# Loads moved from SyncE's to GpSimd's queue, and a transpose moved behind the next row maxima

## The chip, the core and the metric

The kernel runs on one core of a Trainium2 chip. The metric is the device time of one execution in microseconds. The core has TensorE (PE in the profile: matrix products), VectorE (DVE), ScalarE (ACT), GpSimd (POOL) and SyncE (SP, which here only issues DMAs), each working through its own list of instructions in order.

## The reference

Two layers are applied to x of shape (8, 32, 32, 512), all in float32. The second layer is where the change lies; S is 1024 pixels of an image, C is 512.

```python
# layer 0: group norm, 8-head self-attention over the 1024 pixels of an image, residual
x = x + softmax(q k^T) v @ w_out + b_out          # q, k, v from group_norm(x) @ w_qkv + b_qkv
# layer 1: deformable attention
x_ln   = layernorm(x)
q      = x_ln (channels first, re-read as rows of 512) @ wq + bq
o      = gelu(depthwise_conv_7x7_stride_2(q) + dw_b)       # 16 x 16 points per image
grid   = ref_points + tanh(conv_1x1(o))
interp = bilinear_sample(x, grid)                           # 256 sampled rows per image
k = v  = interp @ wv + bv
attn   = softmax((q @ mq_w + mq_b)(k @ mk_w + mk_b)^T)      # 8 heads of 64, 256 keys
msa    = (attn @ (v @ mv_w + mv_b)) @ mo_w + mo_b
z      = msa + x
out    = gelu(layernorm(z) @ mlp_w + mlp_b) + z
```

## The kernel before

The first pass does layer 0 for all images; it leaves in DRAM the rows `mid` (the layer's output), the normalised rows `hat_d` and, for the first images, the convolution's sums `o_d`. The second pass is layer 1 and begins after 2.1 ms. Only the second pass is changed.

**Units.** The second pass goes through 16 half images `hi` of 512 query rows, and each half image through 4 pairs of heads. One pair of one half image is a unit; the units are numbered n = 0 to 63 and are called U0 to U63 here. `unit_steps` (line 1219) makes, for its pair: the scores against 256 keys on TensorE (tile `sc`), the row maxima on VectorE (`nmax`, two instructions), the exponentials on ScalarE (`e`), their transposes on VectorE (`sq`, two), a trip of the transposed tile through DRAM (`sq_d`, `et`), the reciprocal sums (`rs`, `rsT`, through DRAM into `inv`), the product with the values on TensorE (`av`, in the next unit), and its scaling on VectorE into `attH`.

**Behind the attention.** `back_steps` (line 1111) takes a finished half image 128 rows at a time, one such block t per unit. Its steps: `fetch` (DMA of the residual rows into `xr`), `add` (GpSimd adds a bias row to `xr`), `joined` (four-step product `mm<-wo,attH` on TensorE, sum with `xr` into `z` on VectorE, statistics `stats` and `mv`, with one power on GpSimd), `norm` (`zn` on VectorE), `away` (four DMAs `zn_d<-zn` into DRAM), `back` (the DMA `zn<-zn_d`, which brings the tile back with its 32x32 blocks exchanged), `blocks` (VectorE transposes within the blocks: `zT<-zn`), `mlp` (the product `mm<-wm,zT` on TensorE), `biased` (`res` on VectorE), `gelu` on ScalarE, and `end` (GpSimd adds `z` and stores). In the last block or so of the pass TensorE makes the turn instead, without `blocks`.

**Beside it.** For images 6 and 7 the depthwise convolution is made during the units. `conv_steps` (line 1248) runs it in two lanes: lane 0 is five taps per unit on VectorE (two in three of every eight units), each one instruction of `chunk<-pad,dww,chunk`; lane 1 is seven taps per unit, a product on ScalarE (`parts`) and an addition on GpSimd (`chunk<-parts,chunk`). `conv_fetch` (line 950) loads a `hat` for each of eight chunks. `point_steps` (line 1273) finds the sampling points of the next image once per eight units: `conv_load` (line 954) loads the sums `o`, some 24 very small VectorE instructions find the corners, GpSimd gathers rows (`row`, four indirect DMAs), and VectorE weighs them into `smp` (four instructions, in two units of every eight). `fetch_hat` (line 1078) loads the features `hat_h` of a half image for its query products `mm<-hat_h,wqq`.

**Order.** Every step is filed with a place, a decimal number in units, by `at(place, step)`; `run_due` carries all steps out in the order of their places. A wrapper (`InOrder`, line 54) keeps each engine's instructions in just that order. So the places are the order of each engine's list and of each DMA queue, and every instruction of the second pass stands in the profile under line 54: one goes by the tiles. A tile's pool has a fixed number of buffers; a write into a tile waits until the last reader of that buffer is done.

Within unit n the places that matter here are: scores and maxima n; `joined` n + 0.012; first `sq` n + 0.02; `norm` n + 0.03; `away` n + 0.0301; sums n + 0.039; `back` n + 0.0395; `biased` of the block before n + 0.0392; second `sq` n + 0.04; loading of `et` n + 0.0401; `inv` n + 0.0411; query product n + 0.042; `av` of the unit before n + 0.1; its scaling into `attH` n + 0.2; `blocks` n + 0.21; samples n + 0.22; lane 0 taps n + 0.25 on; `xr` loads n + 0.4 of every second unit; and `mlp` n + 1.03, in the next unit.

Of the kernel before, what the change touches and what calls it, by code (L numbers as in the profile page):

```python
# [17 lines left out]
P = 128  # L18
# [4 lines left out]
NC = C // P  # L23
# [224 lines left out]
def attention_then_deformable_attention(  # L248
# [30 lines left out]
    nc = tc.nc  # L279
# [15 lines left out]
    hat_d = [dram.tile([P, NT, C], F32, tag=f"hat{b}", name=f"hat_d{b}") for b in range(B)]  # L295
# [72 lines left out]
    def at(place, step):  # L368
        due.append((place, len(due), step))
# [9 lines left out]
    o_d = [dram.tile([P, NC, NS], F32, tag=f"o{b}", name=f"o_d{b}") for b in range(B)]  # L379
# [27 lines left out]
    with ExitStack() as l0:  # L407
# [3 lines left out]
        nc = InOrder(tc)  # L411
        NX = 2
        NX_T = 3
        xs = {}
# [380 lines left out]
        for b in range(B):  # L795
# [22 lines left out]
            for hp in range(NHP):  # L818
                for qt in range(NT):
                    n = first + hp * NT + qt  # L820
# [7 lines left out]
                    t = qkv[b, hp]  # L828
# [14 lines left out]
    with ExitStack() as l1:  # L843
        nc = tc.nc
# [9 lines left out]
        nc = InOrder(tc)  # L854
# [93 lines left out]
        chat, room = {}, {}  # L948

        def conv_fetch(b, cb):  # L950
            chat[b, cb] = cvhat.tile([P, NT, P], F32, tag="hat", name="hat", bufs=2)
            nc.sync.dma_start(chat[b, cb], hat_d[b][:, :, ts(cb, P)])

        def conv_load(b):
            room[b, "o"] = cv.tile([P, NC, NS], F32, tag="o", name="o")
            nc.sync.dma_start(room[b, "o"], o_d[b][:, :, :])

        def fill(b, cb, par):
            hat = chat[b, cb]
# [64 lines left out]
        def points(b):  # L1024
            conv_load(b)
            conv_gelu(b)
            offsets(b)
            offsets_turned(b)
            targets(b)
            for h in range(2):  # L1030
                gather(b, h)
                sample(b, h)
# [43 lines left out]
        hat, keys, vals, queries, attH = {}, {}, {}, {}, {}  # L1076

        def fetch_hat(hi):
            hat[hi] = raw.tile([P, NC, C], F32, tag="hat", name="hat_h", bufs=2)
            nc.sync.dma_start(hat[hi], hat_d[hi // 2][:, ts(hi % 2, NC), :])  # L1080

# [24 lines left out]
        def tmp(name, bufs):  # L1108
            return work.tile([P, C], F32, tag=name, name=name, bufs=bufs)

        def back_steps(hi, start, step, tail=False):

            b, half = divmod(hi, 2)
            xs = mid[b].rearrange("(t p e) c -> e t p c", e=2, p=P)[half]
            outs = out_tok[b].rearrange("(t p e) c -> e t p c", e=2, p=P)[half]
            xr, z, zn, zT, res = {}, {}, {}, {}, {}
            n_units = 2 * B * NHP

            def fetch(t):
                xr[t] = tmp("xr", 4)  # L1120
                nc.sync.dma_start(xr[t], xs[t])

            def add(t):
                nc.gpsimd.tensor_tensor(xr[t], xr[t], bo_row, ALU.add)
# [21 lines left out]
            def by_matmul(t):  # L1146
                return tail or start + step * t >= n_units - 1
# [42 lines left out]
            for t in range(NC):  # L1190
                over, eve = (start + step * t >= n_units - i and not tail for i in range(2))
                n, pair = start + step * t, start + step * (t - t % 2)

                ends = (n + 0.0301, n + 0.0395, n + 0.21, n + 1.03, n + 1.0392)
                if eve:
                    ends = (n + 0.61, n + 0.72, n + 0.73) if over else (n + 1.06, n + 1.62, n + 1.625)
                places = (pair - 2.6, pair - 1.45), (n + 0.012, n + 0.03), ends
                if tail:
                    turn = n + 0.15 + 0.005 * (t > 0)
                    places = (n - 0.7, n - 0.6), (n, n + 0.01), (turn, n + 0.25, n + 0.26)  # L1200
                turns = (turned,) if by_matmul(t) else (away, back, blocks)
                steps = (fetch, add), (joined, norm), (*turns, mlp, biased)
                for place, what in zip(sum(places, ()), sum(steps, ())):
                    at(place, lambda t=t, what=what: what(t))


                ends = [t - 1, t] if t % 2 and not tail else [t] if tail else []

                for what, after in (
                    (gelu, 0.27 if tail else 0.735 if over else 1.72),  # L1210
                    (end, 0.28 if tail else 0.74 if over else 2.0125),
                ):
                    for i in ends:
                        at(n + after, lambda i=i, what=what: what(i))
# [33 lines left out]
        def conv_steps():  # L1248
            for lane, chunks in enumerate(((0, 3, 6), (1, 2, 4, 5, 7))):
                free = 0.5 + lane  # L1250
                for k in chunks:
                    b, cb = EARLY + k // NC, k % NC
                    first = next(n for n in range(60) if n + 0.49 > free)
                    fills = [first + 0.49, first + 0.55]
                    at(fills[0] - 1.8, lambda b=b, cb=cb: conv_fetch(b, cb))
                    for par, place in enumerate(fills):
                        at(place, lambda b=b, cb=cb, par=par: fill(b, cb, par))
                        at(place + 0.02, lambda lane=lane, par=par: fill_end(lane, par))
                    unit = int(fills[1]) + 1
                    i = 0  # L1260
                    while i < KS * KS:
                        points = unit % (2 * NHP) in (NHP - 1, NHP, NHP + 2)
                        count = 7 if lane else 2 if points else 5
                        for j in range(count):
                            if i == KS * KS:
                                break
                            place = 0.25 + 0.01 * j if not lane else 0.045 + 0.001 * j if j < 4 else 0.65 + 0.01 * j
                            at(unit + place, lambda b=b, cb=cb, i=i, lane=lane: tap(b, cb, i, lane))
                            free = unit + place
                            i += 1  # L1270
                        unit += 1

        def point_steps(b):
            last = 2 * NHP * b - NHP
            at(last - 3.5, lambda: conv_load(b))
            at(last - 2.035, lambda: conv_gelu(b))
            at(last - 1.465, lambda: offsets(b))
            at(last - 1.36, lambda: offsets_turned(b))
            at(last - 0.959, lambda: targets(b))
            for h, (p0, p1) in enumerate(((-0.28, 0.22), (1.72, 2.22))):  # L1280
                at(last + p0, lambda h=h: gather(b, h))
                at(last + p1, lambda h=h: sample(b, h))
            first = 2 * NHP * b
            for hp, place in enumerate((-0.82, -0.815, 0.185, 1.18)):
                at(first + place, lambda hp=hp: key_step(b, hp))
            for t, place in enumerate((-0.81, 0.18)):
                at(first + place, lambda t=t: value_step(b, t))
# [22 lines left out]
        bq_row = wo = wm = bo_row = bm_row = None  # L1310
        prep()
        fetch_hat(0)
        fetch_hat(1)
        for hp in range(NHP):
            key_step(0, hp)
# [10 lines left out]
        for hi in range(2 * B):  # L1326
            if hi > 1:
                at(NHP * (hi - 1) - 1, lambda hi=hi: fetch_hat(hi))
            if hi + 1 < 2 * B:
                back_steps(hi, NHP * (hi + 1) + 1, 1)  # L1330
            else:
                back_steps(hi, NHP * (hi + 1) + 0.65, 0.1, tail=True)
# [34 lines left out]
```

## Time and profile before

| | us |
|---|---|
| median of 3 runs | 3410.59 (3407.61 to 3411.03) |
| the profiled execution | 3415.02 |
| its span from first to last instruction | 3413.3 |
| PE busy | 3274.7 (96%) |
| DVE busy | 2505.4 (73%) |
| ACT busy | 1776.7 (52%) |
| POOL busy | 1537.2 (45%) |

The profile is one execution; busy times are shares of its span. In a row of a timeline the columns are start in us, duration in us, engine, line, operation, out<-in tiles with shapes, and how many instructions are merged (xN); a bracket gives the idle time of the engine before the first of them and what ended it. A row of waits says which engine waited for what: us in total, how many times, the longest. `SPq` and `POOLq` are the queues of those engines, on which DMAs are issued. The granted TensorE clock was 0.983 of full speed on average.

### The profile page before, as it was taken

To read this page: it belongs to the slowest core of one execution; us is meant where nothing else is said; L and a number is where in the kernel's file an instruction comes from. 1 tells how busy PE (TensorE), PEld (TensorE's weight loads), DVE (VectorE), ACT (ScalarE), POOL (GpSimd) and SP (SyncE) were. 2 spreads that over 40 slices of the span, in tenths; PEclk is the share of its full clock that TensorE was granted. 3 is DMA by queue.
4 is the path that set the end of the run, shared out by engine and by line. 5 is a ranking of instruction groups with operands and counts; after the bars stand their busy time and mean duration, and the time that the engine had idled before them with its cause. 6 is when DMAs were issued, how large, how long until landed. Compare 5 with 4: busy or idle time off the path is not lost. (4 is left out here: it accounts for less than half of the span.)

```text
span 3413.3 us, 59709 instructions
## 1 busy us (share of the span) xinstructions
PE 3274.7 (96%) x21504; PEld 1330.2 (39%) x21504; DVE 2505.4 (73%) x3431; ACT 1776.7 (52%) x3811; POOL 1537.2 (45%) x1903
## 2 busy tenths in 40 slices
PE   7999999999999999999999997989999999989998
PEld 3444444444444444444344343433333333333333
DVE  5776788888888888888888885166757767655664
ACT  3443365576576576576566561245544555544342
POOL 1002226646646746745745663114545354532322
PEclk9999999999999999999999999899999999999999
DMA  5666766766766766766776766466667676777764
GB/s 154 176 178 165 207 179 199 214 175 188 221 178 181 229 183 181 217 189 178 212 195 179 209 183 199 130 183 223 213 195 235 222 225 212 227 226 223 249 212 144
DMA packets 488551, 673.01 MB, mean 197 GB/s; under 512 B 81888, under 2 KB 275424, under 8 KB 486208
## 3 DMA queue, kind: packets, MB, share of 16 engines
q1 hardware_dynamic: 457616, 567.09, 57.7%
q0 software_dynamic: 29488, 100.00, 9.6%
q8 instruction: 171, 2.80, 0.3%
q10 hardware_dynamic: 1152, 2.10, 0.2%
q14 instruction: 124, 1.02, 0.1%
HBM read 261.59 MB, written 138.94 MB: 117 GB/s over the span
## 5 line engine op out<-in xcount | busy, mean ns | idle before, releaser
L54 ACT ACTIVATE e<-sc,nmax 128x1024 f32<-128x1024 f32 (+1 forms) x1024 | 802.4, 797 | 606.6 <-DVE nmax L54 605.0
L54 DVE TENSOR_REDUCE nmax<-sc 128x1 f32<-128x1024 f32 (+1 forms) x640 | 751.2, 1214 | 244.8 <-PE sc L54 244.1
L54 POOL TENSOR_TENSOR oa<-part_x,oa 128x256 f32<-128x256 f32 x852 | 639.1, 750 | 556.0 <-ACT part_x L54 509.6
L54 DVE STREAM_TRANSPOSE sq<-e 128x1024 f32<-128x1024 f32 x640 | 766.2, 1228 | 133.6 <-ACT e L54 113.6
L54 ACT ACTIVATE part_x<-pad_x,dww_x 128x256 f32<-128x256 f32 x852 | 440.6, 544 | 243.3 <-POOL oa L54 242.3
L54 PE MATMUL sc<-k,q 64*64 64x512 f32 x4096 | 516.8, 604 | 12.5 <-ACT e L54 9.3
L54 PE MATMUL av<-et,v 128*64 128x256 f32 x4096 | 501.8, 387 | 18.8 <-DMA et<-sq 8.6
L54 PE MATMUL mm<-xT,wqkv 128*64 128x512 f32 x2048 | 463.7, 595 | 3.2 <-issue 3.2
L54 PEld LDWEIGHTS av<-et,v 128*64 128x64 f32 x4096 | 275.8, 137 | 336.3 <-issue 172.4
L54 POOL TENSOR_TENSOR mv<-mv,minus_half 128x1 f32<-128x1 f32 x128 | 76.4, 597 | 605.8 <-DVE mv L54 605.3
L54 PE MATMUL mm<-wm,zT 128*64 128x512 f32 x1024 | 252.7, 639 | 49.8 <-DVE zT L54 48.7
L54 POOL TENSOR_TENSOR chunk<-parts,chunk 128x256 f32<-128x256 f32 x240 | 180.7, 753 | 207.8 <-ACT parts L54 193.4
L54 PEld LDWEIGHTS sc<-k,q 64*64 64x64 f32 x4096 | 137.9, 132 | 321.8 <-issue 207.5
L54 PEld LDWEIGHTS mm<-xT,wqkv 128*64 128x64 f32 x2048 | 149.6, 138 | 254.5 <-issue 239.4
L54 PE MATMUL mm<-wo,attH 128*64 128x512 f32 x1024 | 235.0, 599 | 3.6 <-DVE pad L54 3.6
L54 DVE SCALAR_TENSOR_TENSOR od<-pad_x,dww_x,od 128x256 f32<-128x256 f32 x276 | 233.7, 847 | 5.5
L54 PE MATMUL mm<-wqkv,xT 128*64 128x256 f32 x2048 | 232.1, 379 | 0.0
L54 PE MATMUL mm<-hat_h,wqq 128*64 128x512 f32 x1024 | 231.2, 593 | 0.0
L54 PE MATMUL mm<-w,attT 128*64 128x512 f32 x1024 | 229.8, 592 | 1.4 <-DVE attT L54 1.4
L54 ACT ACTIVATION_READ_ACCUMULATOR e<-sc,nmax 128x1 f32 x1024 | 209.3, 204 | 0.0
L54 DVE STREAM_TRANSPOSE zT<-zn 128x512 f32<-128x512 f32 x58 | 41.3, 711 | 207.6 <-DMA zn<-zn_d 207.6
L54 ACT ACTIVATE parts<-pad,dww 128x256 f32<-128x256 f32 x240 | 126.6, 549 | 115.9 <-POOL chunk L54 115.7
(165 smaller groups left out, 3402.8 us busy)
## 6 DMA issues: line engine op xcount, KB each, us to landing
et<-sq SPq DMA_DIRECT2D x2048, 128.0 KB, 2.8
sq_d<-sq SPq DMA_DIRECT2D x128, 512.0 KB, 3.8
et<-sq_d SPq DMA_DIRECT2D x128, 512.0 KB, 5.1
inv<-rs_d SPq DMA_DIRECT2D x256, 128.0 KB, 4.6
hat_h<-hat_d SPq DMA_DIRECT2D x16, 1024.0 KB, 7.8
xr<-mid SPq DMA_DIRECT2D x64, 256.0 KB, 5.5
x<-in_x_dram POOLq DMA_DIRECT2D x60, 256.0 KB, 4.5
out_dram<-res POOLq DMA_DIRECT2D x60, 256.0 KB, 3.2
```

The costliest lines, as they stand in the source:

```text
L54: return self.tc.keep_in_program_order(op(*args, **kwargs))
```

## The change

The second pass's loads of `hat` (`conv_fetch`, 8 of them), `o` (`conv_load`, 8), `hat_h` (`fetch_hat`, 14 of 16: all but the first two) and `xr` (`fetch`, 64) are issued on GpSimd's queue and not on SyncE's, at the same places. And `blocks`, the transpose `zT<-zn`, goes from place n + 0.21 to n + 1.011. In VectorE's list it stood behind the scaling into `attH` and ahead of the samples and taps; it now stands behind samples, taps and the two maxima of the next unit, and ahead of that unit's `z`. TensorE's list stays as it was, and ScalarE's too.

```diff
@@ conv_fetch, conv_load
-            nc.sync.dma_start(chat[b, cb], hat_d[b][:, :, ts(cb, P)])
+            nc.gpsimd.dma_start(chat[b, cb], hat_d[b][:, :, ts(cb, P)])
...
-            nc.sync.dma_start(room[b, "o"], o_d[b][:, :, :])
+            nc.gpsimd.dma_start(room[b, "o"], o_d[b][:, :, :])
@@ fetch_hat
-            nc.sync.dma_start(hat[hi], hat_d[hi // 2][:, ts(hi % 2, NC), :])
+            (nc.gpsimd if hi > 1 else nc.sync).dma_start(hat[hi], hat_d[hi // 2][:, ts(hi % 2, NC), :])
@@ back_steps, fetch
-                nc.sync.dma_start(xr[t], xs[t])
+                nc.gpsimd.dma_start(xr[t], xs[t])
@@ back_steps, the places of away, back, blocks, mlp, biased
-                ends = (n + 0.0301, n + 0.0395, n + 0.21, n + 1.03, n + 1.0392)
+                ends = (n + 0.0301, n + 0.0395, n + 1.011, n + 1.03, n + 1.0392)
```

## The prediction

> **What bounds it now.** First I read the busy shares: PE has work in 96% of the span, and in the second pass nothing else comes near (VectorE 66% and GpSimd 42% over 2300 to 3300 us). So what counts there is PE's idle time and slow products. The table of waits over 2300 to 3413 us (engine, line, releaser; us, times, longest) says what the change can touch:
>
> ```profile
> DVE zT L54 <- DMA zn<-zn_d: 207.6, 58, 7.7
> DVE attH L54 <- PE av L54: 59.6, 28, 3.3
> PE mm L54 <- DVE zT L54: 48.7, 18, 6.4
> ```
>
> VectorE loses 207.6 us with `zT` at the head of its list and `zn` still on the way; PE pays 48.7 us of it. Second, PE's timeline where nothing is late (U58):
>
> ```profile
> 3276.16 1.96 PE L54 MATMUL sc<-keys,q 64*64 64x256 f32 x32
> 3278.04 3.65 PE L54 MATMUL mm<-wo,attH 128*64 128x512 f32 x16
> 3281.53 3.60 PE L54 MATMUL mm<-wm,zT 128*64 128x512 f32 x16
> 3284.96 3.60 PE L54 MATMUL mm<-hat_h,wqq 128*64 128x512 f32 x16
> 3288.39 1.89 PE L54 MATMUL av<-et,vals 128*64 128x512 f32 x8
> 3290.21 1.96 PE L54 MATMUL sc<-keys,q 64*64 64x256 f32 x32
> ```
>
> A clean unit is 14.05 us, start to start, and the product that needs `zT` is due 1.88 + 3.49 = 5.37 us after `av` has ended (more where PE has keys, values or a convolution fill in between; call that E). Compare a stalled one, PE's row and VectorE's at the same time:
>
> ```profile
> 2792.17 6.33 PE L54 MATMUL mm<-wm,zT 128*64 128x512 f32 x16 [4.56 <-DVE zT L54]
> ```
> ```profile
> 2791.31 0.71 DVE L54 STREAM_TRANSPOSE zT<-zn 128x512 f32<-128x512 f32 x1 [4.47 <-DMA zn<-zn_d]
> ```
>
> It pays twice: 4.56 us of idle time, and a product of 6.33 us where 3.60 is normal; in 100-us stretches with such stalls the granted clock is 0.95 to 0.97 instead of 1.00. Over the 18 waits the slow products add 21.7 us. The most that removing them all can give is 48.7 + 21.7, some 70 us, or 2.1%.
>
> Third, VectorE's timeline in U9 and U13:
>
> ```profile
> 2383.95 0.69 DVE L54 TENSOR_TENSOR attH<-av,inv 128x512 f32<-128x512 f32 x1 [3.03 <-PE av L54]
> 2387.19 0.71 DVE L54 STREAM_TRANSPOSE zT<-zn 128x512 f32<-128x512 f32 x1 [2.55 <-DMA zn<-zn_d]
> 2387.82 4.69 DVE L54 SCALAR_TENSOR_TENSOR chunk<-pad,dww,chunk 128x256 f32<-128x256 f32 x5
> 2392.43 2.35 DVE L54 TENSOR_REDUCE nmax<-sc 128x4 f32<-128x1024 f32 x2
> ...
> 2463.85 0.71 DVE L54 STREAM_TRANSPOSE zT<-zn 128x512 f32<-128x512 f32 x1 [5.71 <-DMA zn<-zn_d]
> 2464.48 2.59 DVE L54 SCALAR_TENSOR_TENSOR chunk<-pad,dww,chunk 128x256 f32<-128x256 f32 x5
> 2467.00 2.34 DVE L54 TENSOR_REDUCE nmax<-sc 128x4 f32<-128x1024 f32 x2
> 2469.26 0.68 DVE L54 TENSOR_TENSOR z<-mm,xr 128x512 f32<-128x512 f32 x1
> ```
>
> The same five taps take 4.61 us in the first and 2.52 in the second. GpSimd's timeline tells why: in U9 its additions cover the taps, in U13 they end at 2463.84, before the taps begin.
>
> ```profile
> 2383.46 3.17 POOL L54 TENSOR_TENSOR chunk<-parts,chunk 128x256 f32<-128x256 f32 x4 [5.59 <-ACT parts L54]
> 2386.58 2.50 POOL L54 TENSOR_TENSOR xr<-xr,bo_row 128x512 f32<-128x512 f32 x2
> 2389.04 2.67 POOL L54 TENSOR_TENSOR chunk<-parts,chunk 128x256 f32<-128x256 f32 x3
> ```
>
> **The transpose moved.** What goes: `zT` no longer holds samples, taps and maxima up while `zn` travels. The trip takes about 7.1 us from the end of `zn`; ahead of `zT` there are now over 10 us of VectorE's list, so nearly all of the 207.6 us goes. But VectorE isn't the bound: it will wait for `av` instead (`attH` needs it), and PE gains only where `zT` comes sooner.
>
> What comes: `zT` now stands behind X (the unit's samples and taps) and the maxima. After `av` has ended VectorE needs 0.25 us to the start of `attH`, 0.58 for `attH`, X, 2.26 for two maxima (2467.00 to 2469.26), and 0.86 from the start of `zT` to the product's start (2791.31 to 2792.17): 3.95 + X. Against 5.37 + E, PE waits X - 1.42 - E per unit. With X = 0 there is none: `sc` then holds the maxima until 2.0 us after `av`, and 2.0 + 2.26 + 0.86 = 5.12. The wait doesn't depend on earlier units, since `attH` starts from `av` each time. An on-time `zT` of the old order stood right behind `attH`; the new order has 1.42 us of room, and X is more than that wherever there are five taps or samples.
>
> X by rows: five taps 2.52 alone, 4.61 beside GpSimd; samples and two taps 3.6 alone (2445.59 to 2449.80, 4.2 in part covered, is the nearest row), and 4.25 (2296.65 to 2300.90, all covered) + 2.01 (2426.50 to 2428.51) = 6.26 covered. Which? GpSimd's `chunk` additions start 1.5 us after the query product's end (U9), `attH` starts 2.0 after it, and they last 6.7 to 8.3 us with `xr`'s. Without the wait for `zn` the taps fall right under them, in every unit of the convolution. I take the covered values, less 0.8 for samples, where GpSimd issues a DMA in between: 5.4. Up to U41, by the wait formula:
>
> - five taps, E = 0 (U5, 13, 21, 29, 37): 5 × 3.2 = 16
> - samples, E = 0 (U6, 14, 22, 30, 38, 12, 20, 36): 8 × 4.0 = 32
> - five taps, E = 1.91 (U9, 17, 25, 33): 4 × 1.3 = 5
> - two taps, `attH` 0.5 late behind the sampling points' small instructions (U11, 19, 27, 35): 4 × 1.0 = 4
> - other units: E of 5.3 or more covers X, or X is short: 0.
>
> That is 57 of waits; slow products behind the 13 long ones at 1.3 each (before: 15.7 us over 12 waits): 17. Together 74, against 34.3 + 15.7 = 50 in those units before: +24. From U42 there are no taps: four sample units at X = 2.7 alone give 5, trips of `zn` over 10 us perhaps 7, so 12, against 14.4 + 6.0 = 20 before: -8. PE's 2.9 us behind ScalarE's `q` should go too, since the maxima run sooner: -3. Sum +13. `z` stands 0.7 us later in the list, but waits for its product until 5.37 us anyway: 0.
>
> **The loads moved.** SP loses 94 issues (8 + 8 + 14 + 64) of 0.43 to 0.55 us, GpSimd gains as many. The tile views (min/median/max ns) give what one costs on either:
>
> ```profile
> L54 SPq DMA_DIRECT2D xr<-mid x64: 376/492/1967, 2270.1 to 3365.9; - x64
> ```
> ```profile
> L54 POOL DMA_DIRECT2D out_dram<-res x60: 557/584/649, 2360.0 to 3383.3; - x60
> ```
>
> So some 0.6 to 0.8 us each (0.77 for the 1 MB loads of `w`), about 60 us on an engine that is idle for over half of the pass. On SP the 42 us give nothing by themselves: it waits 339.9 us for VectorE's `sq` there. What they do give is that `zn_d` no longer stands behind `xr` and `hat_h` (U43's trip of 14.5 us was such a one); that is in the -8. On GpSimd, what queues behind a load is the power for `mv`, which 1.25 us of `sq` covers while a load takes 0.8, the `chunk` additions, whose reader is a unit away, and the end of `res`; `xr`'s loads are 1.15 units (16 us) ahead of their additions, and land in 3.8 us (`xr` in the first pass) to 7.8. I take 0; the bounds are 11 us more (14 `hat_h` × 0.8 ahead of the power, all uncovered) and 14.7 less (GpSimd's present waits for `xr`, all gone and all on the path).
>
> [...]
>
> **Sum.** +13 on the profiled execution's 3415.0 is 3428; that execution lies 4.4 above the median, so 3424.
>
> **Rivals.** (1) *Faster: the taps don't fall under the additions.* If `parts` come later or GpSimd's loads push the additions back, X is that of lone taps: 1.1 and 2.2 per unit in the first two groups, 0 in the others, so 23 us with no slow products: 27 less than 50, with -11 after U42, so -38: 3373. For it: uncovered rows are common in the old order. Against: there the taps were late by the wait for `zn`. X in the middle between the ends gives 36 us of waits and 12 of slow products, -13 in all: 3397. The sign turns at about three quarters of the way from alone to covered. (2) *Slower still:* samples all covered (X = 6.1), and products after waits of 4 us and more as slow as that of U31 (2.7 us, not 1.3): 6 and 18 on top, +37: 3448. (3) *The loads cost:* GpSimd's loads delay additions and powers, or `xr` lands beside `zn` after U42: 5 to 11 on top of any case. (4) *A stall only changes its place:* 57 + 12 of short waits without slow products, 69 against 70, and -3 for `q`: -4 in all, no change that a measurement can tell from none.
>
> **Chances.** About 0.2%, 6.8 us, is what a measurement can tell. Covered taps with my sum or (2) or (3): 0.52, own range 3418 to 3452. Rival 4 and sums that cancel: 0.16. Rival 1, wholly or by half: 0.32. The range for 8 in 10 runs from 3385, between rival 1 and its half, to 3450.
>
> **What would show it.** In the profile after: `DVE zT <- DMA zn` near 0; `DVE attH <- PE av` some 50 times; `PE mm <- DVE zT` about as large as now, but in 20 to 30 waits of 1 to 4 us, in units that had none; the taps' mean toward 0.9 us and `smp`'s toward 1.1; loads on GpSimd at 0.5 to 0.8 us. I'm wrong if the taps stay at 0.5 to 0.6 us, if PE's waits for `zT` fall under 25 us, or if new waits of PE for `et`, `hat_h` or `xr` appear.

## The result, and the profile after

The changed kernel takes 3451.25 us (median of 4, 3448.63 to 3452.94); the kernel before took 3410.81 in the same runs. The ratio is 1.012 (95% interval 1.0102 to 1.0137): 40 us slower. The forecast was 3424, its range ended at 3450, and so the result lies 1.25 us outside. The sign was forecast; the size is three times the forecast's +13, and next to rival 2 (3448).

The profiled execution took 3449.80 us. From the start of U5 to the start of U63 it needs 1090.6 us, the one before 1051.3: the whole loss is in there. (The second pass of these profiles begins anywhere between 2214 and 2224 us, though the code of the first pass is the same. I therefore compare this interval, which is free of that scatter.)

The waits that were shown of before, now over 2300 to 3448 us, and one that was small before (`nmax`, 16.5 us):

```profile
DVE attH L54 <- PE av L54: 117.6, 44, 3.3
DVE nmax L54 <- PE sc L54: 89.9, 32, 8.3
PE mm L54 <- DVE zT L54: 80.7, 30, 6.5
DVE zT L54 <- DMA zn<-zn_d: 10.3, 6, 4.4
```

VectorE's 207.6 us behind `zn` have become 10.3, as the change wants. But VectorE only waits elsewhere, 58 us more for `av` and 73 more for `sc`, and it is busy 35 us longer (753.8 against 718.3). TensorE's wait for `zT` grew from 48.7 to 80.7 us, in 30 places instead of 18. PE's timeline in U13:

```profile
2444.25 3.65 PE L54 MATMUL mm<-wo,attH 128*64 128x512 f32 x16
2454.22 6.55 PE L54 MATMUL mm<-wm,zT 128*64 128x512 f32 x16 [6.31 <-DVE zT L54]
2460.59 3.61 PE L54 MATMUL mm<-hat_h,wqq 128*64 128x512 f32 x16
```

and VectorE's over the same time and the unit after:

```profile
2444.33 0.65 DVE L54 TENSOR_TENSOR attH<-av,inv 128x512 f32<-128x512 f32 x1
2444.91 1.50 DVE L54 TENSOR_SCALAR smp<-row,wt 128x512 f32<-128x512 f32 x1
2446.44 3.02 DVE L54 SCALAR_TENSOR_TENSOR smp<-row,wt,smp 128x512 f32<-128x512 f32 x3
2449.38 1.80 DVE L54 SCALAR_TENSOR_TENSOR chunk<-pad,dww,chunk 128x256 f32<-128x256 f32 x2
2451.11 2.34 DVE L54 TENSOR_REDUCE nmax<-sc 128x4 f32<-128x1024 f32 x2
2453.38 0.69 DVE L54 STREAM_TRANSPOSE zT<-zn 128x512 f32<-128x512 f32 x1
...
2466.59 5.29 DVE L54 SCALAR_TENSOR_TENSOR chunk<-pad,dww,chunk 128x256 f32<-128x256 f32 x5
2471.81 2.34 DVE L54 TENSOR_REDUCE nmax<-sc 128x4 f32<-128x1024 f32 x2
```

(The rows between the two units are left out.) None of the rows shown has a bracket: VectorE doesn't idle ahead of them, and `zT` has simply to wait its turn. GpSimd's rows beside the five taps:

```profile
2465.49 3.29 POOL L54 TENSOR_TENSOR chunk<-parts,chunk 128x256 f32<-128x256 f32 x4 [9.08 <-ACT parts L54]
2468.74 2.87 POOL L54 TENSOR_TENSOR xr<-xr,bo_row 128x512 f32<-128x512 f32 x2
```

The tile views of the taps and of the moved loads (min/median/max ns; a tap's median before was 485):

```profile
L54 DVE SCALAR_TENSOR_TENSOR chunk<-pad,dww,chunk x144: 465/835/1391, 2263.2 to 3033.2; 128x256 f32<-128x256 f32 x144
```
```profile
L54 POOL DMA_DIRECT2D xr<-mid x64: 536/541/612, 2197.1 to 3409.8; - x64
```

### The profile page after: what moved, and what is told of

The parts are those of the page before. It is cut to its first block, busy times and chain, and to the rows that moved or that the text cites. A ratio compares the mean times of both kernels' runs of the same rounds, so it can differ in the third digit from the quotient of the medians.

```text
span 3448.1 us, 59614 instructions
## 1 busy us (share of the span) xinstructions
PE 3285.4 (95%) x21504; PEld 1339.6 (39%) x21504; DVE 2543.7 (74%) x3431; ACT 1777.4 (52%) x3811; POOL 1603.6 (47%) x1997
## 5 line engine op out<-in xcount | busy, mean ns | idle before, releaser
L54 PE MATMUL mm<-wm,zT 128*64 128x512 f32 x1024 | 267.2, 669 | 81.8 <-DVE zT L54 80.7
L54 POOL TENSOR_TENSOR chunk<-parts,chunk 128x256 f32<-128x256 f32 x240 | 188.7, 786 | 201.4 <-ACT parts L54 187.9
L54 PEld LDWEIGHTS sc<-k,q 64*64 64x64 f32 x4096 | 139.1, 132 | 319.3 <-issue 207.6
L54 PEld LDWEIGHTS mm<-wm,zT 128*64 128x64 f32 x1024 | 85.4, 153 | 255.7 <-issue 229.5
```

What stands on the lines that cost most here:

```text
L54: return self.tc.keep_in_program_order(op(*args, **kwargs))
```

## The experiments

Times are medians; each ratio is to the kernel before on the same chip. In the diffs, `-` is the kernel named and `+` what was run.

**The two halves apart.** First only the four groups of loads, then only the transpose.

```diff
 e1_loads: kernel before, with the four dma_start edits alone (blocks stays at n + 0.21)
 e2_turn:  kernel before, with
-ends = (n + 0.0301, n + 0.0395, n + 0.21, n + 1.03, n + 1.0392)
+ends = (n + 0.0301, n + 0.0395, n + 1.011, n + 1.03, n + 1.0392)
```

> Only the loads are moved to GpSimd's queue; the transpose stays at n + 0.21. If the loss is the transpose standing behind taps, samples and maxima: 3404 to 3418 us, TensorE's waits for zT 40 to 50 us as in the kernel before. If the loads cost (GpSimd's list delayed, descriptors, traffic beside zn's trip): 3435 us or more, with TensorE's waits for zT well over 50 us or new waits for hat_h, xr.

Measured: 3458.41, ratio 1.0136 (1.0115 to 1.0157). This is the second of the two cases, and a miss for the prediction's 0: alone, the loads cost 44 us, more than both edits together.

> Only the transpose is moved to n + 1.011; the loads stay on SyncE's queue. If the transpose's place is the loss: 3443 to 3458 us, TensorE's waits for zT 75 to 90 us, the same units stalling as in the changed kernel (mod 8 = 5, 6, 7 and 2). If the loads are the loss: 3400 to 3418 us.

Measured: 3448.20, ratio 1.0104 (1.0086 to 1.0122). As expected: the transpose alone makes nearly all of the loss, up to U42 in the same units and with the same waits to 0.1 us (but for U13 and U31, 0.2 and 0.4 longer). So 44 and 34 us make 40 together, and why must be seen in the trace of the loads alone. (Its execution took 3469.3 us, 11 more than the median. Against the profile before it loses 31 us from U5 to U43, and 19 behind, where trips of `zn` take up to 13.8 us.) Rows around U10 there, GpSimd, VectorE, PE:

```profile
2400.23 0.56 POOL L54 DMA_DIRECT2D out_dram<-res  x1 [0.30 <-POOL res L54]
2400.78 1.09 POOL L54 DMA_DIRECT2D xr<-mid  x2
2401.86 0.54 POOL L54 DMA_DIRECT2D hat_h<-hat_d  x1
```
```profile
2402.23 0.65 DVE L54 TENSOR_TENSOR attH<-av,inv 128x512 f32<-128x512 f32 x1
2412.80 0.71 DVE L54 STREAM_TRANSPOSE zT<-zn 128x512 f32<-128x512 f32 x1 [9.92 <-DMA zn<-zn_d]
2413.44 2.53 DVE L54 SCALAR_TENSOR_TENSOR chunk<-pad,dww,chunk 128x256 f32<-128x256 f32 x5
2415.88 1.28 DVE L54 TENSOR_TENSOR pad<-mm,bq_row 128x512 f32<-128x512 f32 x2
```
```profile
2416.62 3.82 PE L54 MATMUL mm<-wo,attH 128*64 128x512 f32 x10 [6.28 <-DVE pad L54]
```

and SP's queue at the same place in the kernel before:

```profile
2404.48 0.34 SPq L54 DMA_DIRECT2D zn<-zn_d  x1
...
2410.33 1.08 SPq L54 DMA_DIRECT2D xr<-mid  x2
2411.45 0.43 SPq L54 DMA_DIRECT2D hat_h<-hat_d  x1
```

SP, blocked by the steps ahead in its list, issued these 1.5 MB 6 us after `zn` had been called back. GpSimd is free, and issues them within 2 us of the end of `zn` (2400.2): they travel beside it, and the trip takes 12.6 us where it took 6.4. In the old order the pads of the convolution stand behind that `zT`, and TensorE waits some 6 us for them, in four units (0.4 to 2.0 us before). In the new order the same trip is as late (its load is issued 11.0 us after `zn`), but `zT` is due 14.8 us after `zn` anyway, and taps and pads stand ahead of it. The moved transpose hides most of what the moved loads cost.

```diff
 e8_loads_but_hat_h: as e1_loads, but
-(nc.gpsimd if hi > 1 else nc.sync).dma_start(hat[hi], ...)
+nc.sync.dma_start(hat[hi], ...)
```

> Only the loads moved, transpose at n + 0.21, but hat_h (1 MB, 14 of them) left on SyncE. If hat_h landing beside zn's trip is what made that kernel 44 us slower: zn's trip in U10, 18, 26, 34 falls from 12.6 us to under 9, TensorE no longer waits 6 us for pad, 3410 to 3428 us. If xr's loads do it: still 3440 us or more.

Measured: 3434.74, ratio 1.0066 (1.0049 to 1.0082); between both expectations. The 1 MB loads make half of the 44 us (the trip in U10 falls to 9.0); the rest goes with the other loads.

**The loads in the new order,** three kernels on one chip.

```diff
 r_after:            the changed kernel
 r_turn:             as e2_turn
 e13_turn_but_hat_h: the changed kernel, with hat_h's loads on nc.sync
```

> The changed kernel once more, beside the next two on one chip: 3446 to 3454 us.

> Only the transpose moved, once more. If the loads cost next to nothing in the new order: within 4 us of the changed kernel. If they cost some 5 to 13 us (as with the late product): 3436 to 3446 us.

> The changed kernel with hat_h (1 MB, 14 loads) back on SyncE. What the loads cost in the new order, if anything, should be hat_h landing beside zn's or et's trip: then this equals the kernel with the transpose alone, and TensorE's wait for zT in U43 (4.2 us) falls. If xr does it: as slow as the changed kernel.

Measured: 3449.59, 3445.46 and 3447.29; ratios 1.0107 (1.0089 to 1.0126), 1.0098 (1.0082 to 1.0114) and 1.0106 (1.0088 to 1.0124). The intervals overlap: in this order the loads cost 3 to 4 us, give or take some 8, and what `hat_h` has of it can't be told. In the last of the traces the wait in U43 falls from 4.0 us to 1.7, as expected, but the one in U44 rises from 0.6 to 5.8.

**GpSimd's additions beside the taps.** Lane 1's additions are cut to one of 16 rows of the map, in both kernels, and the rest of its sums is left out; then the bias additions to `xr` are cut to a sixteenth too.

```diff
 e3_narrow_after (changed kernel), e4_narrow_before (kernel before)
-nc.gpsimd.tensor_tensor(acc, to, acc, ALU.add)
+nc.gpsimd.tensor_tensor(acc[:, 0:1], to[:, 0:1], acc[:, 0:1], ALU.add)
 e10_narrow_both: as e3_narrow_after, and
-nc.gpsimd.tensor_tensor(xr[t], xr[t], bo_row, ALU.add)
+nc.gpsimd.tensor_tensor(xr[t][:, 0:SQ], xr[t][:, 0:SQ], bo_row[:, 0:SQ], ALU.add)
```

> The changed kernel, with lane 1's additions on GpSimd made on one of 16 columns of each row block (the convolution's sums of that lane are left out otherwise), so that GpSimd no longer covers the taps and samples, though xr's two additions still may. If covered taps and samples are most of the loss: five taps 2.5 to 3.5 us in place of 5.2, TensorE's waits for zT up to U41 fall from 70 to 15 to 35 us, 3375 to 3400 us in all. If the position behind samples and maxima alone is the loss, whatever they take: over 3430 us.

> The same narrow additions in the kernel before, as the control of the run with narrow additions after. There the taps are often uncovered already, and zn's trip sets the waits: 3385 to 3410 us, waits for zT 25 to 45 us. If it stands above the narrow changed kernel, the change is a gain without the cover; if below, the new place costs by itself.

> The changed kernel with lane 1's additions and xr's bias additions made on a sixteenth of their columns (the rest of both sums is left out), so that no long GpSimd addition stands beside the taps. If a tap waits for the GpSimd instruction beside it: five taps 2.5 us in place of 4.4 with the xr additions whole, samples 0.75 each, waits for zT up to U41 by the formula 1.1 x 5 + 2.1 x 8 + 2 = 24 us, 3368 to 3384 us. If taps are slow for another reason: no faster than the run with narrow lane 1 additions (3396 us).

Measured: 3396.51 (0.995, 0.9932 to 0.9968), 3389.05 (0.9936, 0.9916 to 0.9956) and 3381.95 (0.991, 0.9894 to 0.9927), all three as expected. Narrow additions are worth 58 us in the changed kernel (1.012 to 0.995) and 22 in the one before. So what the change loses by the cover (with the ScalarE waits that go with it) is some 33 to 36 of its 40 us, by the medians and by the ratios; without it the change is near a draw (the intervals overlap), not the gain of rival 1. Five taps still took 4.4 us in the first of them, where the `xr` additions are whole. With both narrow, VectorE and PE in U13:

```profile
2442.54 0.69 DVE L54 TENSOR_TENSOR attH<-av,inv 128x512 f32<-128x512 f32 x1 [3.31 <-PE av L54]
2443.15 2.61 DVE L54 SCALAR_TENSOR_TENSOR chunk<-pad,dww,chunk 128x256 f32<-128x256 f32 x5
2445.68 2.35 DVE L54 TENSOR_REDUCE nmax<-sc 128x4 f32<-128x1024 f32 x2
2447.94 0.70 DVE L54 STREAM_TRANSPOSE zT<-zn 128x512 f32<-128x512 f32 x1
```
```profile
2448.78 3.65 PE L54 MATMUL mm<-wm,zT 128*64 128x512 f32 x16 [0.82 <-DVE zT L54]
```

Five taps take 2.53 us; the formula gives a wait of 2.53 - 1.42 = 1.1, and 0.9 to 1.0 is there from start to start, in four of the five units (2.8 in U6).

**The slow products.** In the 13 units that wait longest up to U39, a copy of the joined product fills the wait.

```diff
 e9_filled: changed kernel, mlp(t), in U6 to U39 where n mod 8 is 5, 6 or 7 (not U29)
-res["ps", t] = project(lambda c: zT[t][:, ts(c, P)], lambda c: wm[:, c, :])
+res["ps", t] = mm_tile()
+... 16 products of attH and wo into it, then the 16 of zT and wm (start=True) over them
```

> The changed kernel; in the 13 units up to U39 in which TensorE waits 3.6 us or more for zT, one more copy of the joined product (16 products, 3.4 us, into the tile that the product with zT then overwrites) is put ahead of it, so that TensorE idles 0.2 to 3.1 us there and not 3.6 to 6.7. If the slow products are the clock falling while TensorE idles over some 3 us: they go (32 us at most 5 left), waits for zT fall by the 45 us of the copies, the sum of both 3415 to 3428 us. If the products are slow for another reason (other engines at work beside them): 3445 us or more.

Measured: 3430.39, ratio 1.0056 (1.0039 to 1.0072): 21 to 22 us faster than the changed kernel, 2 us short of the expectation, with 3.4 us of useless products in each of 13 units. PE in U14, and two rows with the granted clock: the product of U13 in the changed kernel (2454.2 on), then that of U13 here. The columns are the stretch, its length, the busy time of PE, PEld, DVE, ACT and POOL with instructions, the clock, DMA share, GB/s.

```profile
2462.90 7.09 PE L54 MATMUL mm<-wo,attH 128*64 128x512 f32 x32
2469.98 3.65 PE L54 MATMUL mm<-wm,zT 128*64 128x512 f32 x16
```
```profile
2454.20:2460.70 6.50, 6.48 (x18) 2.15 (x20) 3.40 (x8) 2.69 (x12) 0.65 (x2) 0.55 0.75 219
```
```profile
2452.28:2455.76 3.48, 3.48 (x16) 1.20 (x18) 3.34 (x8) 2.77 (x13) 0.72 (x2) 1.00 0.68 186
```

The clock was 0.55 behind 6.3 us of idle time and is 1.00 here, behind the 2.8 us that are left. In these units the slow products fall from 32.3 to 2.4 us, 1.75 of them in U37. VectorE and ScalarE work no less beside the product than before (3.34 and 2.77 of its 3.48 us, against 3.40 and 2.69 of 6.50): the clock made it slow, and not the work beside it.

**What would be faster.** The product with `zT` behind the query product, so due 8.80 us after `av`; and `zT` between taps and maxima.

```diff
 e5_late_mlp_before (n + 0.21, loads on SP), e6_late_mlp_after (n + 1.011, loads on GpSimd),
 e7_late_mlp_turn (n + 1.011, loads on SP), e12_before_maxima_late (n + 0.9, loads on SP):
-ends = (..., n + 1.03, n + 1.0392)
+ends = (..., n + 1.0425, n + 1.0427)
 e11_before_maxima (loads on SP):
-ends = (n + 0.0301, n + 0.0395, n + 0.21, n + 1.03, n + 1.0392)
+ends = (n + 0.0301, n + 0.0395, n + 0.9, n + 1.03, n + 1.0392)
```

> The kernel before, with the product that needs zT (and its eviction) put behind the query product: due 8.80 us after av in place of 5.37. Theory (TensorE's waits for zT and the slow products behind them are all that can be gained, and 3.43 us of other work in front hides most): waits of 48.7 fall to some 10, slow products from 21.7 to under 4, 3350 to 3370 us. Rival (zT only gets later too, since VectorE is behind, so the wait moves along): 3395 us or more.

> The same move of the product in the changed kernel. By the wait formula with 8.80 for 5.37: five-tap units 0, sample units mod 8 = 6 about 0.8 us each, mod 8 = 4 about 3.2 each (attH is late there), one or two units behind the convolution: waits for zT of 80.7 fall to 12 to 20, slow products from 36 to under 8, 3335 to 3360 us. Rival (stall moves along): over 3400 us.

> The transpose at n + 1.011 and the late product, with the loads left on SyncE. If the loads cost little in the new order: within 6 us of the run with the loads moved too. If their cost is only hidden by stalls: 10 us or more faster than it.

> Loads on SyncE; the transpose at n + 0.9, behind samples and taps but ahead of the two maxima. The formula loses the 2.26 us of the maxima: waits are X - 3.68 - E, that is 1.6 in the five-tap units, 2.0 in the sample units mod 8 = 6, 4.4 in those mod 8 = 4, 31 us in all, slow products 8: 3380 to 3405 us. If it is the taps under GpSimd's additions alone that cost, wherever the maxima are: over 3430 us.

> The transpose at n + 0.9 and the product that needs it behind the query product; loads on SyncE. The formula gives 1 us in the units mod 8 = 4 and none elsewhere up to U41; what is left are trips of zn behind the convolution: 3350 to 3372 us, against 3374 for the transpose behind the maxima with the late product.

| | us | ratio |
|---|---|---|
| e5_late_mlp_before | 3395.82 | 0.9946 (0.9929 to 0.9962) |
| e6_late_mlp_after | 3387.49 | 0.9923 (0.9906 to 0.9939) |
| e7_late_mlp_turn | 3374.49 | 0.9898 (0.9876 to 0.9920) |
| e11_before_maxima | 3409.21 | 0.9989 (0.9976 to 1.0002) |
| e12_before_maxima_late | 3379.55 | 0.9897 (0.9878 to 0.9916) |

The waits for `zT` fall nearly as expected (18.0 us in e6, 13.5 in e5), but all the late products gain less than that, because the next thing is late: e5, e6 and e12 miss their ranges by 26, 27 and 8 us, and e5's time is that of its rival. e5's waits:

```profile
PE mm L54 <- DVE zT L54: 13.5, 6, 4.2
PEld av L54 <- DMA et<-sq_d: 29.0, 17, 3.7
PE av L54 <- DMA et<-sq_d: 16.8, 11, 2.8
```

Before, `av` waited 3.1 us for `et` (PE's row); the stalls for `zT` had given `et` its time. In e6, with the loads on GpSimd, PE waits 17.8 us there, in e7 with the loads on SP 10.8. Between these two the loads make 13 us by the medians, but the intervals overlap: a price that the changed kernel's stalls hide is likely, and not shown. e7 and e12 beat the kernel before by 33 to 38 us (1.0%), and the changed one by twice that.

e11 does as the formula says, 1.4 us in the five-tap units and 4.4 in the sample units mod 8 = 4, but the units mod 8 = 6 wait 4.2 and not 2.0, since `attH` starts 1.6 us late there. It comes out level with the kernel before, 4 us above its range.

## Why the prediction was right in sign and short in size

The mechanism is the one predicted: X - 1.42 - E of waiting per unit. What failed are terms of the sum. Measured as start-to-start times of PE's products above those of a clean unit:

| term, us | predicted | measured |
|---|---|---|
| five taps (5 units) | 16 | 19.5 |
| samples, mod 8 = 6 (5) | 20 | 21.2 |
| samples, mod 8 = 4 (3) | 12 | 19.8 |
| five taps behind E = 1.91 (4) | 5 | 7.6 |
| two taps (4) | 4 | 1.5 |
| slow products up to U42 | 17 | 32.5 |
| from U43 on, both kinds | 12 | 20 |
| the same before, all | 70 | 73.5 |
| `q`, `pad`, `et` and others | -3 | -9 |
| change | +13 | +40 |

- **Slow products (15 of the 27 missing).** "13 long ones at 1.3 each" took the mean over all waits of before. The price depends on the wait: in both profiles every wait of 3.2 us or more is followed by a slow product, and of those under 2.3 us none. Behind the waits of 3.6 to 6.7 us in the groups above a product loses 1.7 to 2.9 us, 2.5 in the mean (32.3 over 13). U31's row, shown in the prediction with 6.33 us, was the nearer one; I left it to rival 2.
- **"The wait doesn't depend on earlier units, since `attH` starts from `av` each time" (8 us).** False in U12, U20 and U36. VectorE's `attH` in U12 stands behind the second `sq`, and ScalarE's list makes that late:

```profile
2433.63 0.57 ACT L54 ACTIVATE parts<-pad,dww 128x256 f32<-128x256 f32 x1 [2.80 <-POOL chunk L54]
2434.22 1.28 ACT L54 ACT_TABLE_LOAD   x1
2435.52 1.15 ACT L54 ACTIVATE res<-res 128x512 f32<-128x512 f32 x2
2436.69 1.28 ACT L54 ACT_TABLE_LOAD   x1
2437.98 0.47 ACT L54 ACTIVATE e<-sc,nmax 128x256 f32<-128x256 f32 x1
```

  The maxima had ended at 2432.8, but `e` begins at 2438.0, behind `parts`, a gelu and two table loads. So `attH` starts at 2444.33 with no wait, 1.7 us after its time. With X = 2451.11 - 2444.91 = 6.20, the formula gives 6.20 + 1.72 - 1.42 = 6.5, and 6.5 was measured. The trace of before showed it already: `attH` of U12 starts there 2.2 us after its time, without a bracket.

```profile
2439.90 0.65 DVE L54 TENSOR_TENSOR attH<-av,inv 128x512 f32<-128x512 f32 x1
```

  The 0.8 us taken off X for a DMA between the additions was wrong too in this group.
- **X of five taps (6 us in two rows of the table).** 4.61 was read in U9, where only two additions to `xr` and three of `chunk` lay beside; in the new place two taps meet the long `xr` additions, and X is 5.22.
- **From U43 on (8 us).** Rival 3 in part. The trip of `zn` in U42 took 6.6 us and takes 11.0, with 1.5 MB of loads issued beside it; its stall is 4.2 us. The same loads stand beside the trips in U46 and U54, which take 12.0 and 12.3 us; TensorE then waits 2.8 and 3.2 us, against 1.1 and 1.0 with the transpose alone. SP's freed queue did end U43's trip of 14.5 us, which was counted.
- **The loads at 0.** Right for the changed kernel within what can be told (3 to 4 us, give or take 8). An issue on GpSimd's queue takes 536 to 612 ns for an `xr`, no longer than for `out_dram` (557 to 649), 533 to 561 for a `hat_h` and 910 to 959 for a `hat`. But the reason that I gave was incomplete: GpSimd's idle queue issues early (in U10, with the loads alone moved, 0.6 us behind the end of `zn`, where SP's came 9.4 us behind it), and the loads alone cost 44 us where `zT` stands at the head. The 0 came out because the moved transpose hides this, which I had not foreseen: that is luck.
- **Rival 1** has its condition excluded (a tap's median is 835 ns), and the two kernels with lane 1 narrowed, 3396.5 and 3389.1, show no gain either: its -38 isn't there even with most of the cover gone. **Rival 4** needs waits without slow products; up to U42 these cost 32.5 us.

## What to carry to other kernels

When a step is moved behind others in an in-order list, write down its new due time and the sum of what now stands ahead of it, at the durations of the new neighbourhood and not of the old one, and check which engine's list feeds the first item. Price a stall of the matrix engine with its aftermath: in these two profiles waits past some 3 us cost 1.4 to 3.0 us more. A DMA queue that is blocked is also a schedule: here, moving its loads to an idle queue started them earlier (in U10 by some 9 us), beside the transfer that everybody waited for.

## What the runs showed of the hardware

**VectorE's taps end behind GpSimd's additions.** In the U13 rows above, GpSimd's five additions beside the taps end at 2467.03, 2467.90, 2468.78, 2470.19 and 2471.60 us; the five taps end at 2467.32, 2468.18, 2469.06, 2470.48 and 2471.89: each 0.28 to 0.29 us after one. A tap takes 0.48 alone, some 0.84 beside an addition of 0.8, and 1.38 beside one of 1.45. So in these rows a tap's time goes with the length of the addition beside it. With both additions narrow, the five taps of U13 take 2.53 us, 0.51 each.

**TensorE's clock.** In U13 of the changed kernel, behind 6.3 us of idle time, the granted clock was 0.55, and in the two profiles every wait of 3.2 us or more slowed the next product. Under that, nearly equal waits differ. In the profile before, products behind waits of 2.35, 2.80 and 2.95 us (U13, U23 and U37) took 5.35 us each, at a granted clock of 0.68; the one behind 2.92 us (U14) took 3.65 us, at 1.00. In the changed kernel a product took 3.65 us behind a wait of 2.81 (U47), at 1.00 too. Why these waits differ no run here tests.
